# Turning attention values through DRAM, an earlier gate and query schedule, and one batch turned by TensorE, in a graph and attention kernel

## Chip, cores, metric

One core of one Trainium2 chip. The metric is device time in microseconds (us), lower is better. A kernel was timed in several executions; medians are quoted with the smallest and largest run. A single-core program gives no second die to compare the clock with, so the state of a run is judged by its distance from the fastest run of the same kernel.

## The reference

Two layers over `x` of shape (16, 1024, 256), f32. The change touches the second one only:

```python
fea = x.transpose(0, 2, 1)                       # x: result of layer 0, (16, 1024, 256)
c_adj = mean(fea, axis=1)                        # mean of each row
diff = c_adj[:, None, :] - c_adj[:, :, None]
A = abs(abs(sigmoid(diff) - 0.5) - 0.5) * 2.0
Wg = adj[None] * (A + A.transpose(0, 2, 1)) / 2  # "gate rows"
g = relu(einsum('bcn,bnm->bcm', fea, Wg) * para) # "graph"; its transpose gives the queries
k, v = split(x @ kv_w)                           # keys and values, 4 heads of 64
attn = softmax(q @ k.T * scale)
out = (attn @ v), heads side by side             # (16, 1024, 256)
x = layernorm(x + out)
```

Layer 0 (a graph convolution with two batch norms) holds TensorE until 814 us in this kernel (its last products run from 806.96 for 7.03 us).

## The kernel before

A batch of attention is 8 *subturns*, worked off in pairs. A *turn* is a filler (pieces of the next batch: keys, values, graph products, transposes) and then four steps of scores, exponentials and value products. The pieces are put by hand into subturns; in these traces each engine works off its instructions in the order in which the program gives them. The parts that matter (`...` marks cuts):

```python
def sums(g):                                   # DVE: denominators of the softmax
    ...
    nc.vector.tensor_add(ACC[b, hf, pair], E[g, 0], E[g, 1])   # or ACC += E, twice

def attend(g):                                 # TensorE: e x v, summed in PSUM
    ...
    if cp == NT // 2 - 1:
        t = otp.tile([P, FB], F32, tag=f"ot{pair}", bufs=2 - pair, name=f"ot{g}")
        o = O.pop((b, hf, pair))
        nc.scalar.copy(t, o[0])
        nc.vector.tensor_add(t, o[1], t)       # t: sums of values, channels on the partitions
        OT[b, hf, pair] = t

def finish_a(b, j):                            # two row blocks of 128
    p = ps_t.tile([P, 2, C], F32, tag="t", name="pf")
    for a in range(2):
        for pair in range(NP):                 # TensorE turns them: 4 transposes a piece
            nc.tensor.transpose(p[:, a, ts(pair, P)], OT[b, hf, pair][:, ts(k + a, P)], ident)
    r = ...
    nc.vector.tensor_mul(r, p, rd)             # (views cut) times 1/denominator, from PSUM
    (nc.gpsimd if b < B - 1 else nc.vector).tensor_add(r, r, x1s.pop((b, j)))

def load(b, j): ...                            # SP: yt and xr of batch b+2, four fetches and one
def bn2_q(b, j): ...                           # GpSimd: scale yt, add to it
def rows(b, j): ...                            # DVE: turn yt by 32x32 blocks, add xr
def wg_a(b, i): ...                            # ScalarE: gate row; for odd i a DVE sign step too
def wg_b(b, i):                                # DVE: (t + 1) * adj
    nc.vector.scalar_tensor_tensor(t, t, 1.0, adj_sb[:, i, :], op0=OP.add, op1=OP.mult)
def put_x1, get_x1, x1_v                       # batch 1..15: x1 through DRAM, turned by blocks on DVE
def x1_t                                       # batch 0: x1 turned by TensorE

WG = (2, 3, 2, 1)                              # gate rows of the next batch in subturns 0, 1, 2, 3
KV = (2, 3, 3)                                 # keys, values
QG = (6, 6, 6, 7, 7)                           # graph products in subturns 3 to 7
order = (dens, recips, finish_a, finish_b, x1_v, rows, ln1_a, ln1_b, put_x1, get_x1,
         finish_s, means, load, crow)          # rank of the small pieces within a subturn
```

The DMAs discussed are all issued by one engine, SP, through one queue and in program order.

## Time and profile before

| kernel before | |
|---|---|
| time | 2536.23 us (2535.86 to 2536.95, 3 runs) |
| profiled span | 2538.7 us |
| TensorE, VectorE, ScalarE, GpSimd busy | 97, 70, 41, 35 % |
| end of the first score turn (start of the next filler) | 920.4 us |
| steady stage | 14 batches of 104.1 us |

Here is the busy time by stretch for the four turns of one batch (start and end, length, busy us and instruction count of PE, PEld, DVE, ACT and POOL, granted clock, DMA share, GB/s). The turns are in order those of subturns 2 and 3, 4 and 5, 6 and 7, 0 and 1.

```profile
1542.97:1567.91 24.94, 24.94 (x176) 11.86 (x168) 23.90 (x36) 16.14 (x21) 13.15 (x13) 1.00 0.31 75
1567.91:1595.22 27.31, 27.30 (x175) 10.34 (x168) 20.72 (x40) 8.92 (x11) 9.75 (x10) 1.00 0.20 40
1595.22:1621.84 26.62, 26.62 (x169) 10.44 (x161) 18.08 (x26) 10.58 (x15) 5.94 (x7) 1.00 0.38 89
1621.84:1647.07 25.23, 24.84 (x175) 10.02 (x168) 17.99 (x21) 19.82 (x24) 10.13 (x7) 1.00 0.10 22
```

### The profile page before, as it was taken

How to read it: one execution, taken by the hardware profiler on the slowest of the kernel's cores; microseconds unless marked ns; L12 is line 12 of the kernel's file. 1: busy time of each engine (PE TensorE's matmuls, PEld its weight loads, DVE VectorE, ACT ScalarE, POOL GpSimd, SP SyncE). 2: the span in 40 equal slices, each digit the busy share in tenths (PEclk: the TensorE clock that was granted, in tenths of full speed). 3: DMA queues.
4: the chain of work that ended last, by engine and by line, in shares of the span. 5: the costliest groups of instructions: out<-in, count | busy, mean ns of one | idle time of the engine just before them, and what ended most of it. 6: DMA issues, size and time to landing. Idle time of an engine off the chain costs nothing. (4 is left out here: it accounts for less than half of the span.)

```text
span 2538.7 us, 33394 instructions
## 1 busy us (share of the span) xinstructions
PE 2471.2 (97%) x12573; PEld 1048.0 (41%) x12573; DVE 1765.1 (70%) x2654; ACT 1042.9 (41%) x1325; POOL 876.9 (35%) x766
## 2 busy tenths in 40 slices
PE   8999999998998799999999999999999999999997
PEld 4444444443444333443434434444444344443432
DVE  5545554556767676877778778788687786877656
ACT  2000000004452355463554645646455465554644
POOL 2222223222565222433334324344243342432132
PEclk9999999999999899999999999999999999999998
DMA  3122212230785322223222221232222312222000
GB/s 133 66 83 100 100 66 83 100 115 38 273 326 183 60 57 59 51 59 67 47 55 59 58 64 43 55 69 53 63 46 54 76 38 63 47 59 63 9 14 23
DMA packets 392711, 195.27 MB, mean 77 GB/s; under 512 B 265320, under 2 KB 380640, under 8 KB 385376
## 3 DMA queue, kind: packets, MB, share of 16 engines
q1 hardware_dynamic: 392544, 193.08, 27.0%
q8 instruction: 101, 1.65, 0.3%
q14 instruction: 66, 0.54, 0.1%
HBM read 114.31 MB, written 78.71 MB: 76 GB/s over the span
## 5 line engine op out<-in xcount | busy, mean ns | idle before, releaser
L775 ACT ACTIVATE e<-s 128x1024 f32<-128x1024 f32 x512 | 496.3, 1020 | 537.1 <-PE s L763 488.5
L784 DVE TENSOR_TENSOR acc<-acc,e 128x1024 f32<-128x1024 f32 x384 | 522.2, 1360 | 73.1 <-ACT e L775 41.7
L763 PE MATMUL s<-qT,kT 64*64 64x512 f32 x4096 | 495.6, 599 | 14.8 <-ACT e L775 13.3
L794 PE MATMUL o<-e,v 64*64 64x512 f32 x4096 | 486.8, 590 | 0.0
L737 PE MATMUL pg<-wg,x 128*128 128x512 f32 x960 | 429.0, 595 | 0.0
L846 POOL TENSOR_TENSOR r<-r,x 128x512 f32<-128x512 f32 x60 | 115.7, 1928 | 555.5 <-DVE r L841 352.2
L763 PEld LDWEIGHTS s<-qT,kT 64*64 64x64 f32 x4096 | 147.7, 133 | 312.1 <-issue 251.3
L794 PEld LDWEIGHTS o<-e,v 64*64 64x64 f32 x4096 | 157.1, 133 | 285.1 <-issue 276.5
L602 POOL TENSOR_TENSOR yt<-yt,stq 128x512 f32<-128x512 f32 x120 | 188.6, 1572 | 248.5 <-DMA yt<-yT 243.8
L737 PEld LDWEIGHTS pg<-wg,x 128*128 128x128 f32 x960 | 175.5, 190 | 207.8 <-issue 198.2
L101 ACT COPY u<-pa 128x512 f32<-128x512 f32 x15 | 8.8, 586 | 475.3 <-PE pa L306 475.3
L704 DVE SCALAR_TENSOR_TENSOR wg<-wg,adj_sb 128x1024 f32<-128x1024 f32 x128 | 156.6, 1241 | 57.3 <-ACT wg L700 55.0
L306 PE MATMUL pa<-AhT,x 128*128 128x512 f32 x360 | 161.8, 592 | 0.0
L712 PE MATMUL pk<-x1T,kvw 128*128 128x512 f32 x256 | 118.4, 606 | 1.3 <-DVE x1T L663 1.3
L862 ACT ACTIVATE r<-r,nm,rs_z 128x256 f32<-128x256 f32 x128 | 69.8, 594 | 121.2 <-POOL nm L854 121.2
L723 PE MATMUL pv<-kvw,x1T 128*128 128x256 f32 x512 | 115.8, 380 | 0.8 <-ACT kT L715 0.8
L337 PE MATMUL ph<-agg,SW 128*128 128x512 f32 x240 | 112.8, 592 | 0.0
L306 PE MATMUL pa<-T,sx 128*128 128x512 f32 x240 | 107.9, 592 | 0.0
L745 DVE TENSOR_TENSOR qT<-pg,para_sb 128x512 f32<-128x512 f32 x64 | 44.2, 690 | 86.9 <-PE pg L737 86.9
L306 PEld LDWEIGHTS pa<-AhT,x 128*128 128x128 f32 x360 | 68.4, 190 | 86.1 <-issue 86.1
L723 PEld LDWEIGHTS pv<-kvw,x1T 128*128 128x128 f32 x512 | 94.9, 190 | 14.6 <-ACT kT L715 1.6
L482 PE MATMUL po<-hL,SV 128*128 128x512 f32 x224 | 98.4, 592 | 0.0
(193 smaller groups left out, 3113.6 us busy)
## 6 DMA issues: line engine op xcount, KB each, us to landing
h<-hT SPq DMA_DIRECT2D x28, 1024.0 KB, 4.4
hL<-h SPq DMA_DIRECT2D x28, 1024.0 KB, 9.4
x<-in_x_dram SPq DMA_DIRECT2D x16, 1024.0 KB, 7.2
yT<-y SPq DMA_DIRECT2D x64, 256.0 KB, 2.6
out_dram<-r SPq DMA_DIRECT2D x64, 256.0 KB, 2.2
xr<-in_x_dram SPq DMA_DIRECT2D x62, 256.0 KB, 2.9
yt<-yT SPq DMA_DIRECT2D x240, 64.0 KB, 2.2
x<-x SPq DMA_DIRECT2D x120, 128.0 KB, 2.0
```

What stands on the lines that cost most here:

```text
L306: nc.tensor.matmul(p, xs[n][:, k, :], bs[n][:, k, :], start=(k == 0), stop=(k == KN - 1))
L337: nc.tensor.matmul(p, ws[n][:, ts(f, P)], bs[n], start=True, stop=True)
L602: nc.gpsimd.tensor_tensor(y, y, sc, op)
L704: nc.vector.scalar_tensor_tensor(t, t, 1.0, adj_sb[:, i, :], op0=OP.add, op1=OP.mult)
L712: nc.tensor.matmul(p, kvw[:, k, ts(c, P)], x1Ts[b][:, k, ts(h, FB)], start=(k == 0), stop=(k == CT - 1))
L723: nc.tensor.matmul(p[:, ts(a, C)], x1Ts[b][:, k, ts(j + a, P)], kvw[:, k, C:], start=(k == 0), stop=(k == CT - 1),)
L737: nc.tensor.matmul(pg[b], x1s[b, k // 2][:, k % 2, ts(c, P)], wgs[b, k][:, ts(h, FB)], start=(k == 0), stop=(k == NT - 1))
L763: nc.tensor.matmul(t[r * HD : (r + 1) * HD, h, :], kTs[b, pair][h * HD : (h + 1) * HD, ts(2 * cb + r, HD)], qTs[b, pair, hf][h * HD : (h + ...
L775: nc.scalar.activation(E[g, a], S.pop((g, a)), AF.Exp)
L784: nc.vector.tensor_add(ACC[b, hf, pair], ACC[b, hf, pair], E[g, a])
L794: nc.tensor.matmul(O[b, hf, pair][r][h * HD : (h + 1) * HD, :], vs[b][r * HD : (r + 1) * HD, cb, pair * P + h * HD : pair * P + (h + 1) * HD],
L846: (nc.gpsimd if b < B - 1 else nc.vector).tensor_add(r, r, x1s.pop((b, j)))
```

## The change

Its intent is to take work from TensorE.

1. *Sums of values through DRAM.* Each value tile is written to DRAM and fetched back in 32-row blocks, and DVE turns the blocks. 62 of 64 pieces of four TensorE transposes go.
2. *Schedule.* Gate rows 3, 3, 2 in subturns 0 to 2, and graph products from subturn 2 on (4, 6, 5, 5, 6, 6).
3. *Start.* Batch 1's rows are turned by TensorE, as batch 0's are, and not through DRAM.

```diff
+    o_dram = {(b, h): dram.tile([NT // NH, C, P], F32, ...) for b in range(B) for h in range(NH)}
     x1_dram = {
-        (b, j): ... for b in range(1, B) for j in range(NT // 2)
+        (b, j): ... for b in range(2, B) for j in range(NT // 2)
     }
@@ attend
-                t = otp.tile([P, FB], F32, tag=f"ot{pair}", bufs=2 - pair, name=f"ot{g}")
+                t = otp.tile([P, FB], F32, tag=f"ot{pair}", bufs=1, name=f"ot{g}")
                 nc.scalar.copy(t, o[0])
                 nc.vector.tensor_add(t, o[1], t)
-                OT[b, hf, pair] = t
+                if by_pe(b, hf):               # last half of the last batch
+                    OT[b, hf, pair] = t
+                else:
+                    nc.sync.dma_start(o_dram[b, hf][:, ts(pair, P), :]..., t...)
+        def fetch_o(b, j):
+            t = OB[b, j] = otp.tile([P, 2, C], F32, tag="ob", bufs=1, ...)
+            for q in range(NQ):                # four fetches
+                nc.sync.dma_start(t[q * Q : (q + 1) * Q]..., blk[q]...)
@@ finish_a
+            if by_pe(b, hf):
+                ...                            # TensorE, as before
+            else:
+                p = r
+                nc.vector.transpose(r..., OB.pop((b, j))...)
@@ places
-        WG = (2, 3, 2, 1)
+        WG = (3, 3, 2)
-        QG = (6, 6, 6, 7, 7)
+        QG = (4, 6, 5, 5, 6, 6)
+                    put(b, t + k, fetch_o, b, hf * (KB // 2) + k)
+                if b == 1:
+                    put(b - 2, j + 4, x1_t, b, j)
+                    continue
-        order = (dens, recips, finish_a, finish_b, x1_v, ...)
+        order = (dens, recips, x1_t, finish_a, fetch_o, finish_b, x1_v, ...)
... (finish_a counts as TensorE work only where TensorE turns)
```

The last comment has an effect of its own: the first sum of a turn is placed behind the last piece that counts as TensorE work, so DVE makes this sum ahead of the finish and not behind it.

More of the change, by code (lines that the diff above doesn't have):

```diff
@@ L83, in gnn_norm_attention_kernel @@
     y_blk = [yT_all[b].rearrange("i (d e) (q n) -> q e (i d) n", e=Q, q=NQ) for b in range(B)]
+    o_dram = {(b, h): dram.tile([NT // NH, C, P], F32, name=f"o{b}_{h}") for b in range(B) for h in range(NH)}
     x1_dram = {
-        (b, j): dram.tile([CT, 2 * P, P], F32, name=f"x1_{b}_{j}") for b in range(1, B) for j in range(NT // 2)
+        (b, j): dram.tile([CT, 2 * P, P], F32, name=f"x1_{b}_{j}") for b in range(2, B) for j in range(NT // 2)
     }
@@ L784, in sums, with by_pe @@
                     nc.vector.tensor_add(ACC[b, hf, pair], ACC[b, hf, pair], E[g, a])
+        def by_pe(b, hf):
+            return b == B - 1 and hf == NH - 1
         def attend(g):
@@ L806, in attend @@
                 nc.vector.tensor_add(t, o[1], t)
-                OT[b, hf, pair] = t
+                if by_pe(b, hf):
+                    OT[b, hf, pair] = t
+                else:
+                    nc.sync.dma_start(
+                        o_dram[b, hf][:, ts(pair, P), :].rearrange("i p n -> p i n"),
+                        t.rearrange("p (i n) -> p i n", n=P),
+                    )
         def dens(b, hf):
@@ L830, in recips @@
             )
+        OB = {}
+        def fetch_o(b, j):
+            hf, k = divmod(2 * j, KB)
+            if by_pe(b, hf):
+                return
+            t = OB[b, j] = otp.tile([P, 2, C], F32, tag="ob", bufs=1, name=f"ob{b}_{j}")
+            blk = o_dram[b, hf].rearrange("i (d e) (q n) -> q e (i d) n", e=Q, q=NQ)
+            for q in range(NQ):
+                nc.sync.dma_start(
+                    t[q * Q : (q + 1) * Q].rearrange("p a (d n) -> p (a d) n", n=Q),
+                    blk[q][:, ts(k // 2, 2 * C // Q), :],
+                )
         def finish_a(b, j):
             hf, k = divmod(2 * j, KB)
-            p = ps_t.tile([P, 2, C], F32, tag="t", name="pf")
-            for a in range(2):
-                for pair in range(NP):
-                    nc.tensor.transpose(p[:, a, ts(pair, P)], OT[b, hf, pair][:, ts(k + a, P)], ident)
             pool_r = (rp, "r") if b < B - 1 else (x1p, "x1")
             r = pool_r[0].tile([P, 2, C], F32, tag=pool_r[1], name=f"r_{b}_{j}")
+            if by_pe(b, hf):
+                p = ps_t.tile([P, 2, C], F32, tag="t", name="pf")
+                for a in range(2):
+                    for pair in range(NP):
+                        nc.tensor.transpose(p[:, a, ts(pair, P)], OT[b, hf, pair][:, ts(k + a, P)], ident)
+            else:
+                p = r
+                nc.vector.transpose(
+                    r.rearrange("p a c -> p (a c)"), OB.pop((b, j)).rearrange("p a c -> p (a c)")
+                )
             rd = RD[:, b * NT + 2 * j : b * NT + 2 * j + 2, :].rearrange("p a h -> p (a h)")
@@ L953, in fast, with is_short @@
         nsteps = B * NS
-        order = (dens, recips, finish_a, finish_b, x1_v, rows, ln1_a, ln1_b, put_x1, get_x1, finish_s, means, load, crow)
+        order = (dens, recips, x1_t, finish_a, fetch_o, finish_b, x1_v, rows, ln1_a, ln1_b, put_x1, get_x1, finish_s, means, load, crow)
         rank = {f: k for k, f in enumerate(order)}
-        short = (dens, recips, finish_a, crow)
+        short = (dens, recips, x1_t, crow)
+        def is_short(fa):
+            f, a = fa
+            return f in short or f is finish_a and by_pe(a[0], 2 * a[1] // KB)
         long = (keys, values, graph)
@@ L976, in arrange @@
             few.sort(key=lambda fa: rank.get(fa[0], len(rank)))
-            few_pe = [fa for fa in few if fa[0] in short]
+            few_pe = [fa for fa in few if is_short(fa)]
             order = spread(many, few_pe) if len(many) < len(few_pe) else spread(few_pe, many)
@@ L983, in arrange @@
             for fa in few:
-                if fa[0] not in short:
+                if not is_short(fa):
                     at_ = 0
@@ L1083, in fast @@
             now = [p for s in (2 * t, 2 * t + 1) for p in [(opening, (s,))] + arrange(at.get(s, []))]
-            behind = max((k + 1 for k, fa in enumerate(now) if fa[0] in short), default=0)
+            behind = max((k + 1 for k, fa in enumerate(now) if is_short(fa)), default=0)
             for k in range(len(now) + 1):
```

## The prediction

> **What bounds the kernel now.** I read the page's busy shares first, then the busy times by stretch, to see whether the bound is the same throughout.
>
> ```profile
> PE 2471.2 (97%) x12573; PEld 1048.0 (41%) x12573; DVE 1765.1 (70%) x2654; ACT 1042.9 (41%) x1325; POOL 876.9 (35%) x766
> ...
> 1416.60:1518.10 101.50, 101.10 (x655) 41.77 (x653) 79.50 (x118) 53.55 (x65) 38.57 (x36) 1.00 0.26 58
> ```
>
> The second line is one batch of the attention stage (columns: stretch, length, busy us of PE, PEld, DVE, ACT, POOL, clock, DMA share, GB/s). TensorE is busy 101.1 of 101.5 us at the full clock, DVE 79.5. So in the steady stage TensorE's instruction stream is the time, and only what leaves that stream can shorten it. A batch is 8 subturns, taken two at a time: one turn is a filler (keys, values, graph matmuls, transposes) and then four score and value steps. The timeline of PE shows what a piece to be removed costs there (start, length, what; pipelined ends overlap, so I use differences of starts).
>
> ```profile
> 1491.64 0.66 PE L837 MATMUL pf<-ident,ot 128*128 128x128 f32 x4
> 1492.14 6.17 PE L737 MATMUL pg<-wg,x 128*128 128x512 f32 x14
> ...
> 1526.66 0.60 PE L837 MATMUL pf<-ident,ot 128*128 128x128 f32 x4
> 1527.10 1.89 PE L723 MATMUL pv<-kvw,x1T 128*128 128x256 f32 x8
> 1528.92 1.95 PE L763 MATMUL s<-qT,kT 64*64 64x512 f32 x16
> 1530.69 1.90 PE L794 MATMUL o<-e,v 64*64 64x512 f32 x16
> 1532.97 2.01 PE L763 MATMUL s<-qT,kT 64*64 64x512 f32 x16 [0.39 <-ACT e L775]
> ```
>
> Four transposes hold the stream 0.50 or 0.44 us, mean 0.47. The last line is the only wait of a batch: after the filler of subturns 0 and 1 the second score group waits 0.39 us for ScalarE, which is late because it makes gate rows there.
>
> TensorE's idle time lies at the ends. After the load of weights the timelines of DVE, PE and the SP queue show this:
>
> ```profile
> 874.62 0.71 DVE L656 STREAM_TRANSPOSE x1T<-xb 128x512 f32<-128x512 f32 x1 [5.75 <-DMA xb<-x]
> 883.79 0.71 DVE L656 STREAM_TRANSPOSE x1T<-xb 128x512 f32<-128x512 f32 x1 [5.15 <-DMA xb<-x]
> 885.63 0.37 PE L683 MATMUL pc<-ident,cs 128*8 128x128 f32 x1 [9.82 <-DVE cs L666]
> 886.31 4.19 SPq L651 DMA_DIRECT2D xb<-x  x8
> 890.60 0.38 SPq L686 DMA_DIRECT2D crow_d<-crow  x1
> 908.46 1.98 PE L763 MATMUL s<-qT,kT 64*64 64x512 f32 x8 [3.13 <-ACT e L775]
> ```
>
> Batch 1's turned rows come back from DRAM; DVE, in order, waits 5.75 and 5.15 us for them, so the means (cs) come late and TensorE waits 9.82 us. Then the row of means (crow) waits in the SP queue behind eight fetches.
>
> **What the Trainium skill says.** "VectorE: DVE Perf Modes", section "The three transpose paths", says that TensorE turns a full 128 by 128 into PSUM, while VectorE turns only 32 by 32 blocks: hence the way through DRAM, which puts the blocks in place. The trace agrees with the cost of the DVE half: 705 ns for 128x512 in the groups by line. "DMA: Bandwidth & Descriptors", section "Why small descriptors are slow (HBM only)", gives small packets a fixed cost each; the fetches here have 128-byte rows. The trace has 265320 packets under 512 B of 392711, yet a DMA share of 0.26, so there is room. "Perfetto Trace Analysis", section "Identifying the Most-Contended Engine", warns that matmul busy time overstates nearness to the roofline; I use PE's 97% only as "the stream has no gaps", which the starts above confirm.
>
> **The change part by part.**
>
> *Values through DRAM.* Of 64 pieces of four transposes 62 go (the last half of the last batch keeps its two). In their place DVE turns 62 blocks (62 x 0.705 = 44 us more, 1765 to about 1809), and SP issues 62 writes of 256 KB and 248 fetches of 64 KB. Which of the 62 x 0.47 = 29 us counts?
> - In subturn 1 ScalarE ends the wait. Its chain from the end of the last value group at 1518.3: dt copied at 1519.9, then by starts 2.15 us for each even row, 1.05 for each odd, 0.47 a copy. Before, 5 rows, 5 copies and 1.0 us of waits for keys bring the first exponential to 1531.9. With WG = (3, 3, 2) it is 6 rows (6.45 + 3.15 = 9.6) and 5 copies (2.35): 1531.9 again, because the extra row fills the waits. The second score group still starts at about 1532.9, so the 14 pieces of this place in batches 1 to 14 gain nothing; the wait merely grows from 0.39 to some 0.9 us.
> - The 4 pieces that fall in the last batch have no filler beside them and are covered by the end below.
> - The other 44 are in a gapless stream: 44 x 0.47 = 20.7 us.
>
> *Does a DRAM wait come back?* The value tile is whole about 1.35 us after the turn's end; a write of 256 KB takes 2.6 us to land, four fetches take SP 0.49 us each and the last lands 2.2 to 3.0 us later: 8 to 9 us after the turn. In subturn 1 DVE, held by gate rows, reaches the block at about 10.5 us: no wait. In subturn 5 it arrives at 7.4 (rows, statistics, reciprocals, the first sum) and waits 1 or 2 us, but after that DVE has some 23 us of work in a turn of 24 and the exponentials have buffers for three steps: TensorE should not see it. The second block of each half has a whole turn.
>
> *Gate rows and queries.* The graph matmuls start at subturn 2 (4, then 6), so the eighth gate row is wanted a subturn earlier. In the turn that began at 1543.4, DVE began gate rows 8.1 us in; with the 0.7 us block ahead of them and no odd row but the last, row 8 is ready at 11.7, while PE reaches it after values (5.2) and 7 graph products (6.0), at 11.3. I book 0.3 us x 14 = -4.2 us. In itself the moved filler saves nothing: it is the same work in the same stream.
>
> *Batch 1 turned by TensorE.* Adds 16 transposes (4 x 0.47 = 1.9 us) and four PSUM copies, takes away eight writes, 16 fetches and the 10.9 us of DVE waits. The graph product of batch 0 ends at 875.8; with three of the new pieces it ends at 877.3, the means being ready by then. So pc comes at 877.8 in place of 885.6 and the first scores at 878.5 in place of 887.4 (gain 9). The row of means now leaves at once: from the issue of crow_d at 890.6 to ScalarE's use at 896.5 is 5.9 us, so it arrives at 884.5 in place of 896.5. ScalarE then needs 12.0 us (6 rows, 5 copies) to the next exponential: the score group of 908.46 starts near 897.5. Gain 11 us.
>
> *The end.* In the last batch there is no filler, and ScalarE stands behind the finish of batch 14:
>
> ```profile
> 2472.95 1.90 PE L794 MATMUL o<-e,v 64*64 64x512 f32 x16
> 2479.63 2.84 PE L763 MATMUL s<-qT,kT 64*64 64x512 f32 x12 [4.79 <-ACT e L775]
> ```
>
> DVE's finish now comes after the first sum (1.15) and a transpose (0.65), and the block before it waited for DRAM, which makes the sums of that turn about 2 us late. So this wait grows by some 3.5 us, against two removed pieces worth about 1: -2.5 us.
>
> Sum: 20.7 - 4.2 + 11 - 2.5 = 25.0 us. 2536.2 - 25.0 = 2511.
>
> **The rivals.**
> - *The DRAM trip becomes the wait.* If fetches land at 12 us and not at 9, DVE is late in every turn that has a first block, the eighth gate row comes 2 or 3 us late, and TensorE waits some 2 us x 29: all of the steady gain and more is lost, time about 2535 to 2560. For it: before, the issue of a 128 KB write at 865.56 came back turned on DVE at 874.62, 9 us. Against: those fetches stood behind a load in the queue, and the fetch of values is issued first after its write.
> - *TensorE is freed everywhere* (ScalarE absorbs its row, no gate row is late): 62 x 0.47 = 29, start 11, end 0: 2496.
> - *DVE becomes the bound.* With 82 of 100 us it is not on average, but the turn of subturns 2 and 3 has DVE at 23.9 of 24.9 before, and the sum of DVE work there grows by 0.7. If this turn is DVE's, it lengthens by about 0.5 us each: 14 x 0.5 = 7 us off, 2518.
> - *The start gains nothing* (the eight PSUM banks or the key copies hold it): 2522.
>
> **Range and chances.** The 20.7 is arithmetic on a gapless stream and safe if DVE keeps up; the -4.2 can be 0 to -14, the start 5 to 12, the end 0 to -4. Together 2500 to 2527. Faster by over 2% would need under 2485.5, below even the best rival; slower by over 2% needs a wait in each turn of over a microsecond beyond my first rival. Both are small.
>
> **What would show it.** Right: PE busy down by about 26 us; the starts of subturn 5 to 7 fillers shorter by 0.44 to 0.50 and a steady batch near 100.4 us in place of 101.5; the wait of the second score group up to about 0.9 us and not gone; the first scores near 878 and crow_d issued at once; the DVE block transposes waiting 1 to 2 us in subturn 5 only. Wrong: PE waits for wg of over 0.5 us in each batch, or long DVE waits for ob in subturn 1, or a start of scores still after 885.

## The result

| | median us | range | runs |
|---|---|---|---|
| before | 2536.59 | 2535.86 to 2539.43 | 4 |
| after | 2563.15 | 2561.01 to 2565.30 | 4 |

The ratio is 1.0103 (95% interval 1.0085 to 1.012). It is the mean time of one kernel's fast runs over that of the other's of the same rounds, so not quite the ratio of the medians. Within 2%, but 1% *slower* where 1% faster was predicted, and far outside the range of 2500 to 2527. The mechanism was wrong, not only a size.

The busy line of the page after:

```profile
PE 2443.5 (95%) x12341; PEld 1022.5 (40%) x12341; DVE 1817.5 (71%) x2716; ACT 1039.9 (41%) x1325; POOL 828.9 (32%) x766
```

The busy time by stretch after, for the four turns of the same batch, and their sum (columns as above):

```profile
1542.44:1573.26 30.82, 28.40 (x180) 12.91 (x172) 27.14 (x38) 15.12 (x20) 14.68 (x14) 1.00 0.28 69
1573.26:1597.37 24.11, 24.11 (x168) 9.06 (x160) 18.78 (x38) 8.92 (x11) 6.85 (x9) 1.00 0.39 77
1597.37:1622.70 25.33, 24.66 (x160) 9.23 (x153) 17.65 (x27) 10.56 (x15) 2.94 (x5) 1.00 0.32 84
1622.70:1647.84 25.14, 24.39 (x172) 9.68 (x164) 20.45 (x23) 20.66 (x25) 12.03 (x9) 1.00 0.38 74
sum 105.40, PE 101.56 PEld 40.87 DVE 84.03 ACT 55.27 POOL 36.49; mean PE 25.39 PEld 10.22 DVE 21.01 ACT 13.82 POOL 9.12
```

PE's busy time fell by 27.7 us, as predicted (26). The time rose all the same: in this batch PE worked 101.56 of 105.40 us, so 3.84 us of gaps took the place of 0.4. Most are in the first turn. Its timeline of PE before (start, length, engine, line, operation, count; in brackets the idle time and what ended it):

```profile
1543.49 0.66 PE L837 MATMUL pf<-ident,ot 128*128 128x128 f32 x4
1543.99 5.34 PE L723 MATMUL pv<-kvw,x1T 128*128 128x256 f32 x24
1549.17 5.43 PE L737 MATMUL pg<-wg,x 128*128 128x512 f32 x12
```

And after:

```profile
1542.96 5.45 PE L724 MATMUL pv<-kvw,x1T 128*128 128x256 f32 x24
1548.25 5.31 PE L738 MATMUL pg<-wg,x 128*128 128x512 f32 x12
1555.25 1.12 PE L738 MATMUL pg<-wg,x 128*128 128x512 f32 x2 [1.69 <-DVE wg L705]
1557.11 2.84 PE L738 MATMUL pg<-wg,x 128*128 128x512 f32 x6 [0.74 <-DVE wg L705]
```

The four transposes are gone from the head, and the graph products now wait 1.69 + 0.74 us for gate rows from DVE. In the view of waits of PE after (waiting for what, total us, times, longest) the two largest are:

```profile
PE pg L738 <- DVE wg L705: 32.3, 25, 2.4
PE pc L684 <- DVE cs L667: 15.1, 14, 2.2
```

Besides, the keys (`pk`) wait 0.75 us a batch for x1T, in place of 0.39 us for ScalarE in the same turn.

The whole account over the profiled spans (2563.4 - 2538.7 = +24.7), from the starts of the fillers after the first score turn (920.44 before, 905.69 after) and 14 batches later (2376.32 and 2395.69):

| stretch | predicted | measured |
|---|---|---|
| up to the end of the first score turn | -11 | -14.75 |
| 14 steady batches | -20.7 + 4.2 = -16.5 | +34.1 |
| last batch and tail | +2.5 | -0.4 + 5.7 = +5.3 |

So the miss is in the steady stage. The rise of 34.1 there is made up so (14 batches):

- transposes gone: 56 x 0.47 = -26.2;
- waits of PE: for gate rows 32.3, for the means 15.1, for x1T 14 x (0.75 - 0.39) = 5.0: +52.4;
- a wait that stood on the weight loads in the kernel before and is gone: about -12.9 (shown with e3);
- stretches of half clock (0.50 for 3.4 us at a time, six places, one of them double), estimated to cost half their length: +11.9;
- not attributed: about +9. Some 6 of it may be lost overlap, by an estimate: in the lines above a group runs on for 0.16 us past the next start (1543.99 + 5.34 against 1549.17), a wait is counted only from that end, and there are 39 waits more (25 + 14 + 14 - 14).

The start, by the same lines as the prediction shows for before:

```profile
874.99 1.09 PE L764 MATMUL s<-qT,kT 64*64 64x512 f32 x8
...
893.71 3.47 PE L764 MATMUL s<-qT,kT 64*64 64x512 f32 x16 [3.12 <-ACT e L776]
```

The means, which follow the last transposes of batch 1 at once (874.78), are turned without the wait of 9.82 us, and the group that started at 908.46 starts at 893.71. The row of means left at 875.43 in place of 890.60.

### The profile page after: what moved, and what is told of

It reads as the page before. It is cut to its first block, busy times and chain, and to the rows that moved or that the text cites. A ratio compares the mean times of both kernels' runs of the same rounds, so it can differ in the third digit from the quotient of the medians.

```text
span 2563.4 us, 33445 instructions
## 1 busy us (share of the span) xinstructions
PE 2443.5 (95%) x12341; PEld 1022.5 (40%) x12341; DVE 1817.5 (71%) x2716; ACT 1039.9 (41%) x1325; POOL 828.9 (32%) x766
## 5 line engine op out<-in xcount | busy, mean ns | idle before, releaser
L785 DVE TENSOR_TENSOR acc<-acc,e 128x1024 f32<-128x1024 f32 x384 | 503.1, 1310 | 101.2 <-ACT e L776 73.9
L764 PE MATMUL s<-qT,kT 64*64 64x512 f32 x4096 | 493.1, 597 | 12.7 <-ACT e L776 11.9
L738 PE MATMUL pg<-wg,x 128*128 128x512 f32 x960 | 444.8, 610 | 32.3 <-DVE wg L705 32.3
L603 POOL TENSOR_TENSOR yt<-yt,stq 128x512 f32<-128x512 f32 x120 | 168.1, 1401 | 445.8 <-DMA yt<-yT 384.5
L705 DVE SCALAR_TENSOR_TENSOR wg<-wg,adj_sb 128x1024 f32<-128x1024 f32 x128 | 172.0, 1345 | 53.6 <-ACT wg L701 51.3
L878 POOL TENSOR_TENSOR r<-r,x 128x512 f32<-128x512 f32 x60 | 82.4, 1373 | 359.5 <-DVE r L873 191.5
L713 PE MATMUL pk<-x1T,kvw 128*128 128x512 f32 x256 | 119.4, 610 | 11.7 <-DVE x1T L657 10.4
L812 DVE TENSOR_TENSOR ot<-o,ot 128x512 f32<-128x512 f32 x64 | 44.1, 689 | 91.8 <-ACT ot L811 91.6
L66 POOL TENSOR_SCALAR rs_a<-mv_a 128x2 f32<-128x2 f32 x64 | 19.8, 310 | 251.6 <-DVE mv_a L552 228.5
```

Of the source, the lines that this page charges most:

```text
L603: nc.gpsimd.tensor_tensor(y, y, sc, op)
L713: nc.tensor.matmul(p, kvw[:, k, ts(c, P)], x1Ts[b][:, k, ts(h, FB)], start=(k == 0), stop=(k == CT - 1))
L738: nc.tensor.matmul(pg[b], x1s[b, k // 2][:, k % 2, ts(c, P)], wgs[b, k][:, ts(h, FB)], start=(k == 0), stop=(k == NT - 1))
L764: nc.tensor.matmul(t[r * HD : (r + 1) * HD, h, :], kTs[b, pair][h * HD : (h + 1) * HD, ts(2 * cb + r, HD)], qTs[b, pair, hf][h * HD : (h + ...
L785: nc.vector.tensor_add(ACC[b, hf, pair], ACC[b, hf, pair], E[g, a])
```

## Experiments

Each kernel ran 3 rounds beside the kernel before on the same chip (three chips: e1 to e4, e5 to e8, e9 to e11), gave correct results and had a profile. The kernel before had medians of 2537.2 to 2538.2 us. All at a glance:

| run | what | median us | ratio to before (95%) |
|---|---|---|---|
| e1 | batch 1 by TensorE only | 2527.17 | 0.9958 (0.9941 to 0.9974) |
| e2 | values through DRAM only | 2567.35 | 1.0116 (1.0099 to 1.0133) |
| e3 | schedule only | 2528.09 | 0.9963 (0.9947 to 0.998) |
| e4 | DRAM and batch 1, old schedule | 2554.75 | 1.0067 (1.0051 to 1.0084) |
| e5 | e4 with the load ahead of the values | 2530.54 | 0.9973 (0.9957 to 0.999) |
| e6 | only the queue traffic of the DRAM way | 2554.93 | 1.0066 (1.0049 to 1.0083) |
| e7 | only the added DVE transposes | 2562.77 | 1.0100 (1.0084 to 1.0117) |
| e8 | e1 + e3, no DRAM | 2515.61 | 0.9912 (0.9896 to 0.9929) |
| e9 | after with the load ahead of the values | 2545.63 | 1.0027 (1.001 to 1.0043) |
| e10 | e9, one finish later | 2543.34 | 1.0021 (1.0004 to 1.0038) |
| e11 | e8, one finish later | 2508.62 | 0.9884 (0.9868 to 0.9901) |

### The three parts alone

Theory 1 held that the earlier want for the eighth gate row (the schedule) made the waits; theory 2, that the way through DRAM did, whatever the schedule.

**e1, batch 1 only.**

```diff
+                if b == 1:
+                    put(b - 2, j + 4, x1_t, b, j)
+                    continue
-        order = (dens, recips, finish_a, ...
+        order = (dens, recips, x1_t, finish_a, ...
... (batch 1's DRAM tiles go; x1_t counts as TensorE work)
```

> The kernel before with one part of the change alone: batch 1's rows turned by TensorE, not through DRAM. In the profile of the changed kernel the start was 14.8 us earlier by the end of the first score turn. If that start belongs to this part, this run is 13 to 17 us faster than the kernel before (about 2521) and its steady turns are unchanged (24.9, 27.3, 26.6, 25.2 us). If the early start needs the new gate rows or the value path, the gain is below 5 us.

Measured 2527.17, some 10 us faster, less than the 13 to 17 expected. The filler after the first score turn starts at 910.28 in place of 920.44, and the steady turns did not change. This part does what it was meant to. The rest of the 14.75 us comes with the other parts: by the same count e8 gains 12.6 and e4 15.6 us. Why is not shown.

**e2, DRAM only** (old `WG` and `QG`, batch 1 as before).

```diff
-                OT[b, hf, pair] = t
+                    nc.sync.dma_start(o_dram[b, hf]..., t...)
-                    nc.tensor.transpose(p[...], OT[b, hf, pair][...], ident)
+                nc.vector.transpose(r..., OB.pop((b, j))...)
```

> The kernel before with the sums of values through DRAM alone, old gate rows and queries, batch 1 as before. Theory 1 (the 2.4 us waits for gate rows 7 and 8 in each batch come from the new schedule asking for them a subturn earlier than a later DVE can give): no PE wait for wg, and the run gains, 2515 to 2535. Theory 2 (the DRAM trip or DVE's extra 44 us makes DVE late wherever it stands): PE still waits 2 us or more per batch, for wg, cs or x1T, and the run is slower than before, 2545 to 2565.

Measured 2567.35: slower by 30 us by itself, beyond even theory 2's band. PE waits for the sixth gate row (the six graph products of subturn 3 use rows 1 to 6) 39.6 us in 13 waits, though the row is wanted as late as in the kernel before. The timeline of PE in e2, one batch:

```profile
1563.57 1.48 PE L738 MATMUL pg<-wg,x 128*128 128x512 f32 x2 [3.06 <-DVE wg L705]
```

The clock behind it is halved (columns as above; 0.50 is the clock):

```profile
1564.20:1567.60 3.40, 3.40 (x16) 0.81 (x18) 3.26 (x7) 2.71 (x4) 3.20 (x4) 0.50 0.24 78
```

That of GpSimd (POOL) in e2, in the same batch:

```profile
1536.36 2.50 POOL L603 TENSOR_TENSOR yt<-yt,stq 128x512 f32<-128x512 f32 x2 [28.55 <-DMA yt<-yT]
```

This line is a clue that no theory had named: GpSimd stands 28.55 us waiting for a fetch that has nothing to do with the values.

**e3, schedule only.**

```diff
-        WG = (2, 3, 2, 1)
+        WG = (3, 3, 2)
-        QG = (6, 6, 6, 7, 7)
+        QG = (4, 6, 5, 5, 6, 6)
```

> The kernel before with the new gate rows and queries alone. Theory 1 in its strong form (the schedule alone is too early for DVE): PE waits for wg near 2 us per batch, 2560 to 2575. In its weak form (it needs the value path's DVE work too): wait for wg under 1 us per batch, 2532 to 2550. Theory 2 has no wait for wg here and no change of time beyond 5 us.

Measured 2528.09, 9 us *faster*, outside every band named. The cost of 4.2 us that the prediction put on this part is a gain, and it is a gain of a wait that PE's busy time had hidden. The waits of PEld (weight loads) in the kernel before:

```profile
PEld pd L815 <- DVE acc L784: 12.9, 14, 1.0
PEld pf L837 <- DVE acc L784: 10.6, 13, 0.8
PEld pg L737 <- DVE wg L704: 8.8, 13, 0.7
```

Only the first is a wait in full. Weight loads of `pf` stand idle 0.81 us elsewhere too, with no cause named, and the last two lines remain in e3 (12.2 and 13.0 us). The first of them in e3:

```profile
PEld pd L815 <- DVE acc L784: 0.8, 1, 0.8
```

In the kernel before, the eight products `pd` at the start of the turn of subturns 4 and 5 wait, once in each batch, some 0.9 us for DVE's last sum. The timeline of PE shows that group as busy throughout:

```profile
1568.42 2.12 PE L815 MATMUL pd<-acc,ones 128*32 128x512 f32 x8
```

Only the timeline of PEld shows the wait, at the second set of weights, inside that group:

```profile
1569.49 0.14 PEld L815 LDWEIGHTS pd<-acc,ones 128*32 128x32 f32 x4 [0.92 <-DVE acc L784]
```

In the kernel after the same group takes 1.06 us. The new schedule moves 4 graph products a batch (3.44 us) into the turn in which DVE has its 23.9 us of work, so DVE finishes in time. Turn lengths in e3 are 28.65, 24.55, 24.89, 25.13, in all 103.2 against 104.1 us. So DVE *already* bound one turn of the kernel before.

**e4, DRAM and batch 1, old schedule.**

```diff
-        WG = (3, 3, 2)
-        QG = (4, 6, 5, 5, 6, 6)
+        WG = (2, 3, 2, 1)
+        QG = (6, 6, 6, 7, 7)
```
(against the kernel after)

> The changed kernel with the old gate rows and queries: values through DRAM and batch 1 by TensorE. Theory 1: the sum of the two parts, 2500 to 2520, faster than both kernels, half-clock windows in the steady stage gone. Theory 2: 2530 to 2550.

Measured 2554.75, just above theory 2's band; PE waits 40.4 us for gate rows. Theory 1 fell: without the new schedule the waits are longer, not shorter. What e4 leaves is a cost of the DRAM way of 27.6 us (2554.75 - 2527.17 of e1), on top of the 62 x 0.47 = 29 us of transposes that it saves and does not get.

### What in the DRAM way costs

Two explanations stood. A: the writes of values hold the SP queue, so the next batch's load comes late and its GpSimd work falls where DVE makes gate rows. B: DVE's added work alone. For A speaks the SP queue's timeline, before:

```profile
1504.42 1.98 SPq L435 DMA_DIRECT2D yt<-yT  x4
```

and after:

```profile
1519.27 0.38 SPq L816 DMA_DIRECT2D o<-ot  x1
1521.58 1.91 SPq L853 DMA_DIRECT2D ob<-o  x4
1523.53 2.08 SPq L436 DMA_DIRECT2D yt<-yT  x4
```

and the queue's own view of waits after, whose largest entry is new:

```profile
SPq L816 <- DVE ot L812: 723.7, 62, 23.8
```

The writes wait 11.7 us each at the head of the queue (723.7 / 62). The load behind them used to be issued a whole turn ahead and now comes some 20 us later: 19.4 us before the filler of subturns 2 and 3 (1523.53 against 1542.96), in place of 39.1 (1504.42 against 1543.49). In e2 it is 18.9 (1531.89 against 1550.77). In the kernel before, GpSimd was through with this scaling at 1512.8; now it works in the same microseconds as DVE. GpSimd after:

```profile
1527.50 3.18 POOL L603 TENSOR_TENSOR yt<-yt,stq 128x512 f32<-128x512 f32 x2 [27.17 <-DMA yt<-yT]
```

DVE beside it, and its next, undisturbed gate row:

```profile
1529.69 1.53 DVE L698 TENSOR_SCALAR wg<-wg 128x1024 int32<-128x1024 int32 x1
1531.26 2.19 DVE L705 SCALAR_TENSOR_TENSOR wg<-wg,adj_sb 128x1024 f32<-128x1024 f32 x1
...
1535.56 0.69 DVE L698 TENSOR_SCALAR wg<-wg 128x1024 int32<-128x1024 int32 x1
1536.28 1.23 DVE L705 SCALAR_TENSOR_TENSOR wg<-wg,adj_sb 128x1024 f32<-128x1024 f32 x1
```

The same two instructions take 1.53 and 2.19 us beside GpSimd, 0.69 and 1.23 us without: 1.8 us a batch. The Trainium skill, "SBUF — State Buffer", section "Who interferes with whom", says that a DVE instruction with two inputs in SBUF contends with a GpSimd instruction that reads SBUF, over a shared port pair. The trace agrees for the gate row, which has two (the row and `adj_sb`).

**e5, the load ahead of the values.** Writes are issued only when the fetch is due, and `load` is ranked before it. The amount of DVE work is unchanged, but not its order: the new rank also moves the sixth gate row ahead of two statistics on DVE.

```diff
@@ attend (against e4)
-                    nc.sync.dma_start(o_dram[b, hf]..., t...)
+                OT[b, hf, pair] = t
@@ fetch_o
+            if k == 0:
+                for pair in range(NP):
+                    nc.sync.dma_start(o_dram[b, hf]..., OT.pop((b, hf, pair))...)
-        order = (..., finish_a, fetch_o, ..., means, load, crow)
+        order = (..., finish_a, load, fetch_o, ..., means, crow)
```

> The run with values through DRAM, batch 1 by TensorE and the old gate rows (2554.7 us, wait for gate rows about 3.1 us in each batch), with one difference: the writes of value tiles are issued only when their fetch is, and behind the load of the next batch's rows, so that they no longer hold this load at the head of the SP queue. Theory A (the held load puts GpSimd's scaling of these rows beside DVE's finish and gate rows, where the two slow each other): the scaling of the first rows is back before the turn, the wait for gate rows falls below 1 us a batch, the half-clock windows of the steady stage go, 2505 to 2525. Theory B (DVE's added work of 0.7 us a block, with a product that reads SBUF and not PSUM, makes it late by itself): the wait stays over 2 us a batch, 2540 to 2555.

Measured 2530.54, above A's band by 5 us, but 24 us less than e4, for an order of issue (the ratios to the kernel before, 1.0067 and 0.9973, give the same 24). All waits of PE for gate rows are gone, and the scaling is early again. GpSimd in e5, which by then runs some 16 us ahead of the kernel before:

```profile
1495.27 4.22 POOL L603 TENSOR_TENSOR yt<-yt,stq 128x512 f32<-128x512 f32 x2 [11.53 <-DVE acc L785]
```

So A holds in e4, with two reservations. First, the moved gate row helps as well. In e5 DVE ends it at 9.1 us after the start of the filler, and PE comes to it at 9.6; behind the two statistics (1.1 us) it would end at 10.2. So by this estimate some 0.6 of the 3.1 us a batch is the order on DVE, and the rest is DVE's earlier entry into the turn (its step on the value tile starts 0.9 us in, against 3.7 in e4). Second, the clock: e4 has 13 stretches of half clock in the steady stage, two of them double, and e5 has none. At half their length they cost some 26 us, about as much as the whole gain, so much of what the early load saves is clock that followed the long waits.

And 2530.54 is still above e1's 2527.17: even so the DRAM way saves nothing. A new wait has come, for ScalarE, which stands behind GpSimd's part of the finish. PE in e5:

```profile
1543.52 2.00 PE L764 MATMUL s<-qT,kT 64*64 64x512 f32 x16 [1.69 <-ACT e L776]
```

ScalarE (ACT) in e5, just before:

```profile
1540.43 1.09 ACT L894 ACTIVATE r<-r,nm,rs_z 128x256 f32<-128x256 f32 x2 [4.58 <-POOL nm L886]
```

PE waits 1.69 us there and 0.88 us in the turn of subturns 0 and 1 in each batch (0.75 for x1T and 0.13 for ScalarE, against 0.38 before), together 2.2 us more; the four pieces removed are worth 4 x 0.47 = 1.9.

**e6, queue only.** TensorE still turns; the tiles are written and fetched as in the change, and the fetched data are overwritten unused.

```diff
                 OT[b, hf, pair] = t
+                if b < B - 1:
+                    nc.sync.dma_start(o_dram[b, hf]..., t...)
+        def fetch_o(b, j): ...                 # into the tile that finish_a overwrites
```

> The kernel before with the writes and fetches of values added and their result thrown away (the fetch fills the tile that the product then overwrites; batch 15 has none), TensorE still turns the values, DVE has no added work. Theory A: wait for gate rows of 1.5 us or more a batch, 2550 to 2575. Theory B: under 0.5 us a batch, 2532 to 2545.

Measured 2554.93, 17 us slower: inside A's band. But the wait of PE for gate rows is only 0.9 us (11.5 in 13 waits), little more than half of what A asked for. The turn of subturns 2 and 3 grows from 24.93 to 25.88 us, which is 13 us of the 17. The trace shows A's mechanism with DVE's own work unchanged: GpSimd waits 29.14 us for the load, scales at 1531.95, and DVE's instructions beside it are slow. DVE in e6:

```profile
1535.09 1.53 DVE L698 TENSOR_SCALAR wg<-wg 128x1024 int32<-128x1024 int32 x1
1536.65 2.18 DVE L705 SCALAR_TENSOR_TENSOR wg<-wg,adj_sb 128x1024 f32<-128x1024 f32 x1
```

(The fetch also takes one of the two `r` buffers a subturn earlier than the finish did; no run separates that.)

**e7, DVE only.** No DMA; one more DVE block transpose before each product, whose result is overwritten.

```diff
+            if not (b == B - 1 and hf == NH - 1):
+                nc.vector.transpose(r..., x1s[b, j]...)
             nc.vector.tensor_mul(r, p, rd)
```

> The kernel before with one added DVE block transpose in each finish (62 of them, its result overwritten by the product), TensorE still turns the values, no DMA added. Theory A: wait for gate rows up to 1 us a batch, 2535 to 2552. Theory B: 2 us or more a batch, 2560 to 2585.

Measured 2562.77, 25 us slower: B's band, though the wait (19.2 us in 13) is under the 2 us a batch that B asked for. In the timeline of PE in e7:

```profile
1561.08 1.13 PE L737 MATMUL pg<-wg,x 128*128 128x512 f32 x2 [1.47 <-DVE wg L704]
```

The turn of subturns 2 and 3 is 26.55 us long in place of 24.93, 14 x 1.6 = 23 us of the 25; the other three turns stay within 0.1. So each of A and B costs PE time by itself where TensorE still has its transposes. Both act through DVE's lateness in one turn. This may be why they have no fixed share each, and why e5 clears the gate rows in the old schedule with DVE's added work still there; e5 differs from e7 also in the order on DVE, in the transposes gone from PE and in PE's new waits in the turn before, which give DVE time, so this is argued and not shown.

### Can it be mended?

**e8, e1 and e3 together, no DRAM.**

```diff
 (the edits of e1 and e3)
```

> The kernel before with the two parts that gained alone, batch 1 by TensorE (-10 us) and the new gate rows and queries (-9 us), and no values through DRAM. If they act in different places, the sum: 2514 to 2522, faster than both kernels. If the new gate rows delay the start that batch 1 gains (one more row ahead of the second exponential), 2520 to 2527.

Measured 2515.61. The gains add up: 10 + 9 is 19 and it is 22. The prediction booked 11 - 4.2 = 6.8 us on these two parts, and 20.7 on the third, which loses.

**e9, the kernel after with the load first** (e5's edit on it).

```diff
-        order = (..., finish_a, fetch_o, ..., load, crow)
+        order = (..., finish_a, load, fetch_o, ..., crow)
 (and the writes in fetch_o, as in e5)
```

> The changed kernel whole (new gate rows and queries) with the load of the next batch's rows ahead of the writes of values in the SP queue. Both causes found act in it, the held load and DVE's added work; this takes the first away. If the held load was most of the 2.4 us wait for gate rows in each batch, the wait falls under 1 us and the time to 2505 to 2525, below the kernel before. If DVE's added work is most of it, the wait stays over 1.5 us and the time is 2535 to 2555.

Measured 2545.63, 17.5 us better than the kernel after (19 by the ratios) but still slower than before: in the band of "DVE's work is most". Its waits of PE:

```profile
PE pg L738 <- DVE wg L705: 19.1, 26, 0.7
PE pc L684 <- DVE cs L667: 15.9, 14, 2.7
```

Both name DVE. The held load is thus most of the damage in the old schedule (24 of 27.6 us), but about two thirds in the new one (17.5 of the 26.6 us by which the kernel after is slower than before); e9 does not get the moved gate row of e5, so the two shares are not quite comparable. With DRAM and the load first the new schedule *costs* 14 to 15 us (e9 against e5); without DRAM it gains 9 (e3). It seems to take up the slack of DVE that the DRAM way needs.

**e10, e9 with a later finish.** The profile of the kernel after shows one wait of 8.80 us in the last batch, where the scores stand behind ScalarE's finish of the batch before:

```profile
2500.61 3.69 PE L764 MATMUL s<-qT,kT 64*64 64x512 f32 x16 [8.80 <-ACT e L776]
```

```diff
-                    put(b, t + 2 + k + late, finish_b, b, ...)
+                    put(b, t + 2 + k + late + (k if hf == NH - 1 and b < B - 1 else 0), finish_b, b, ...)
```

> The same, and ScalarE's last step of the finish of a batch's last two row blocks one subturn later, behind the exponentials of that turn. In the last batch TensorE waited 8.8 us for ScalarE, which stood behind this step (4.8 us in the kernel before). If this step is the cause, that wait goes and the run is 5 to 9 us faster than the run above; if it is DVE's lateness, under 2 us.

Measured 2543.34, about 2 us less, and the intervals overlap: inconclusive as a time. In the profiled runs the wait is gone and the last batch with the tail is 8.9 us shorter (157.8 in place of 166.7 us), as expected. But the 14 steady batches are 7.7 us longer, with waits for the means up from 15.9 to 23.3 us. Why these grow is not shown.

**e11, e8 with that later finish.** The edit is the same as in e10.

> The best so far (batch 1 by TensorE and the new gate rows, values turned by TensorE, 2515.6 us) with the same later step. The 4.8 us wait in the last batch goes: 2509 to 2513. Nothing else changes.

Measured 2508.62 (2507.68 to 2509.58), ratio 0.9884: just under what was expected, and the fastest of all. Here the wait (4.79 us before) goes and nothing takes its place, which fits DVE having room there.

## Why the prediction was wrong

**Right.** PE's busy time down by about 26 us (27.7); DVE up to about 1809 (1817.5); the first scores near 878 and the row of means sent at once (874.99 and 875.43); the late finish in the last batch (+3.5 us named, +4.0 measured: 4.79 to 8.80). In the turn of subturns 0 and 1 the removed piece indeed gained little (25.23 to 25.14 in this batch), though not by the named wait: that for ScalarE vanished and one of 0.75 us for x1T stood in its place. And where no wait came, the removed piece did count: the turn of subturns 4 and 5 fell by 3.2 us (27.31 to 24.11), which is 1.72 of products moved away, 1.05 of the wait at `pd` and 0.44 of transposes.

**Wrong, the step that failed: "a gapless stream: 44 x 0.47 = 20.7 us" with "The last line is the only wait of a batch".** It read idle time on PE alone. The wait of PEld for DVE at `pd`, 12.9 us, sat inside PE's busy groups. With DVE at 23.90 of 24.94 us, the turn of subturns 2 and 3 was bound by DVE and PE *together*. The prediction saw the 23.9, wrote of it as a rival, and booked 0.5 us a batch on it; e7 shows 1.6. In place of a gain of 20.7 us the steady stage brought 52.4 us of waits, and the sign of being wrong that the prediction had set, waits for gate rows of over 0.5 us a batch, came true (2.4). The Trainium skill, "Perfetto Trace Analysis", section "Identifying the Most-Contended Engine", says that the share of matmul busy time is not a good measure of how close TensorE is to its roofline. Nor did 97% mean a stream without waits here.

A smaller misreading: the window of 101.50 us that the prediction takes for a batch starts 2.4 us inside one. A batch runs from 1414.16 to 1518.26, 104.1 us. No sum of the prediction rests on this.

**Wrong, the step "row 8 is ready at 11.7".** The turn began at about 1542.9 after, and the eighth row was done when DVE started its next instruction at 1556.97: 14.1 us. DVE entered the turn late. Its timeline after, with the last step of the value tile and the eighth row:

```profile
1546.70 0.68 DVE L812 TENSOR_TENSOR ot<-o,ot 128x512 f32<-128x512 f32 x1
...
1555.83 1.23 DVE L705 SCALAR_TENSOR_TENSOR wg<-wg,adj_sb 128x1024 f32<-128x1024 f32 x1
```

In the kernel before that step starts at 1545.22. Counted from the first instruction of the filler (1543.49 before, 1542.96 after), it is begun 1.7 us in before and 3.7 us in after. The turn ahead of it had been given one more gate row and the 0.70 us block, and its instructions beside GpSimd took 1.8 us more. The prediction took DVE's start from the old trace. The term of 4.2 us became 32.3 us of waits, and the part "schedule" that it was booked under gains by itself (e3).

**Wrong by omission: what else waits in the SP queue.** The rival "The DRAM trip becomes the wait" had nearly the right size (2535 to 2560) but the wrong path. It asked when the fetched values arrive; in the steady batch shown here DVE waits for them 0.20 us, and in all 14.5 us in 13 waits, the longest 3.9. It did not ask what stands *behind* the write. The Trainium skill, "DMA: Bandwidth & Descriptors", section "Two DMAs through the same engine are not ordered", tells the author to make the issuing engine wait on the first DMA's semaphore before it issues the dependent one. The trace shows such waits (59.5 us of SP for `o<-ot` before the fetches), and 723.7 us more for tiles not yet made; e5 and e9 show that the new order of issue is worth 24 (with the reservations above) and 17.5 us.

**Mis-sized.** Start 11, measured 14.75 (e1 alone: 10). The end cost 5.3 us and not 2.5, by the tail, where a new wait of 2.76 us for DVE's last sum and stretches of half clock stand.

**Open.** Stretches of half clock follow the longer waits. In e2 and e4 there is one in each of the 13 batches with a wait of 2.5 to 3.6 us; in the kernel after there are six in 14 batches, four behind waits for gate rows (2.3 to 3.1 us, mostly in two pieces) and two after waits of 2.19 and 1.97 us for the means; there are none in e5 (1.69), e6 (up to 1.2) and e7 (1.47). In e9 and e10 there are two each, after waits for the means of 2.00 to 2.99 us, while waits of 2.22 and 2.33 us in e10 have none. So length alone does not decide. This is a correlation across kernels, and no run set the length of a wait by itself. Also open is where the rest of the 9 us of the steady account is, and how A and B divide the loss of the kernel after, since both act through the same lateness.

## What to carry to other kernels

Before moving work from a full engine to one that is "only 70% busy", look at the target's busy time turn by turn, and at the waits of the weight loads and not only of the matmuls: an engine can bind one turn in four and be invisible in every average. Before adding a DMA to an in-order queue, ask what is issued behind it and when its source is ready; issue independent loads first. Split a change into its parts and run each alone: here two parts gained 22 us together (29 with one further move) and the third lost 30.

## What the Trainium skill lacked or had wrong

- "DMA: Bandwidth & Descriptors", section "Two DMAs through the same engine are not ordered": says to wait on the issuing engine, but not what this does to later, independent DMAs of that engine, and no page gives its size. Here the writes waited 11.7 us each at the head of the queue, and a load behind them was issued some 20 us later; issuing it first took 24 us off a kernel of 2555.
- "Perfetto Trace Analysis", section "Identifying the Most-Contended Engine": it lacks that a wait can show on the weight loads only. 12.9 us of waits for DVE sat in groups of `pd` that the matmul view shows as busy for 2.12 us in place of 1.06.
- "SBUF — State Buffer", section "Who interferes with whom": the trace agrees for two SBUF inputs (a 128x1024 f32 gate row 2.19 us in place of 1.23 beside GpSimd). The one-input sign step on 128x1024 int32 also took 1.53 in place of 0.69 us there. The page says that such a step can contend only in a two-port mode; whether this one was in such a mode no run here shows.
- "TensorE: Matmul & The Clock Gate", section "HAM oscillation — how this bites in real kernels": gives as the rule no idle gaps above some 3.4 us. Here stretches of half clock of 3.4 us each followed every wait of 2.5 to 3.6 us for a gate row (13 of 13 in e2 and in e4), and some shorter ones (six in the kernel after, behind waits of 1.7 to 2.4 us), so gaps below the rule's figure were not safe. None followed the waits of up to 1.69 us in e5 and e7. The length of one stretch agrees with the page's window of some 3.4 us.
- "VectorE: DVE Perf Modes", section "The three transpose paths": its times are for 128x128 bf16, so the prediction's "the trace agrees with the cost" had no such figure to agree with. The f32 block transpose of 128x512 took 0.70 us here, and the TensorE way 0.44 to 0.50 us of the stream for four 128x128 f32 transposes.
